# x1 transposed by DMA, its gain and shift on VectorE, the keys' statistics a block ahead, and the output's sums ahead of Q

## The chip, the cores and the metric

One of the eight cores of a Trainium2 chip runs the whole kernel; nothing is shared with another core. The metric is the time on the device in microseconds (us), as the median of several executions.

## What is computed

The input src is 4 batches of 2048 rows with 256 numbers. Each row is first normalized; then two branches are computed from it and multiplied:

```python
xn = _layernorm(src)
# branch 1: linear attention with 16 heads of 64, then a feed-forward net (FFN)
q = xn @ Wq + bq ; k = xn @ Wk + bk ; v = xn @ Wv + bv
Q = elu(q) + 1 ; K = elu(k) + 1
KV = einsum('bshd,bshm->bhdm', K, v)                    # a sum over all rows of the batch
Z = 1 / (einsum('bshd,bhd->bsh', Q, K.sum(axis=1)) + EPS)
o = einsum('bshd,bhdm,bsh->bshm', Q, KV, Z)
x1 = layer_norm(xn + o @ Wo + bo) * g1 + be1
y  = gelu(x1 @ W1 + b1) @ W2 + b2                       # 256 -> 1024 -> 256
s  = layer_norm(x1 + y) * g2 + be2
# branch 2: a gated net whose operands are rounded to FP4 in blocks of 16
g  = silu(fp4_linear(silu(fp4_linear(xn, w_gate)) * fp4_linear(xn, w_up), w_down))
out = src + s * g
```

All matrix products run in float32.

## The kernel before

**Blocks and batches.** The rows are taken in 32 blocks of 256 (two tiles j of 128 rows): 8 blocks in each of 4 batches. Attention of a batch needs sums over all of the batch's keys, so the keys of batch b + 1 are worked on beside the blocks of batch b. Each block of the first three batches (0 to 23) takes two key blocks along (`subs`). In blocks 0 to 3 of a batch, they are new: x is loaded (`x_k`), statistics are taken (`keys_stats`), x is normalized (`keys_norm`, the tile xn_k), stored, and transposed to xnT_k. In blocks 4 to 7 xn and xnT are read back from DRAM for the second half of the key columns. Keys are prepared one block ahead, so new ones are prepared in blocks 1, 2, 7 to 10 and 15 to 18 (and, a little differently, in block 0). In blocks 24 to 31 there are no keys left.

**The transposes of the keys** are done by DMA, in three steps. `keys_apart` has ScalarE copy the two 16-bit halves of each float32 number apart from each other (`apart<-xn_k`). A transposing DMA on SP's queue turns the eight 128x128 squares of 16-bit numbers (`apartT<-apart`). In `keys_T` one ScalarE copy puts the halves together again (`xnT_k<-apartT`).

**One block n of the loop**, in TensorE's order: keys times Wk (pk), the denominators of attention (pz), the sums of keys with xn (pxk), gate and up of block n + 1 (pg), down of block n (pd), the second key block's pk, attention of block n (pa, giving x1), the second pxk, W2's product of block n - 1 (py, 28 matmuls of 128x128, of which the trace records two passes each; a product of two 2x2 block matrices in seven multiplications instead of eight), and inside it, after its first 20 matmuls, the transposes of x1 (pt_x) and of the FP4 scales (pscale; in the last batch after 26), then Q of block n + 1 (pq) and W1's product of block n (pf). So x1 of block n has to be normalized and transposed between pa and pf.

**x1 before the change.** `attention_norm` takes the mean and variance on VectorE (`st`, `mv`), adds epsilon (`rstd`), raises to the power -1/2 on GpSimd (L430) and normalizes with one tensor_scalar for each tile. g1 and be1 are not in this x1: `x1_T` transposes it on TensorE with four 128x128 matmuls into PSUM, and ScalarE multiplies by g1 and adds be1 as columns when it copies the result to x1T. The same x1 in rows gets g1 and be1 + b2 (the row tile `shift`) later, in `ffn_addend` on GpSimd, so that it can be added to W2's product in `output`.

**The output of block n - 1.** `output` (called after Q of block n + 1 is issued) adds the product's seven partial sums to x1 with five VectorE additions (`add_seven`, into the tile s, reading PSUM), takes statistics of s, normalizes and gates it (`output_of`) and stores it.

**What sets the order.** TensorE's instructions stand in the order of the program (`keep_in_program_order`). Those of VectorE, ScalarE, GpSimd and SP's queue are placed by the framework's scheduler from the blocks on; `tc.issue_after(ins)` forbids it to place an instruction before another. Each engine and SP's queue of DMAs then works strictly in the order it got. PSUM has four banks for passing products (`mm_tile`); a product takes a bank that an earlier one has given back, so a late reader on ScalarE or VectorE can hold a later product. In Q, VectorE's clamp (`zq<-e,pq`, the maximum of product and clipped exponential) is such a reader.

Of the kernel before, what the change touches and what calls it, by code (L numbers as in the profile page):

```python
# [8 lines left out]
F32 = mybir.dt.float32  # L9
# [6 lines left out]
P = 128  # L16
# [6 lines left out]
def linear_attention_gated_by_fp4_ffn(  # L23
# [116 lines left out]
    def as_rows(v):  # L140
        return v.rearrange("(o f) -> o f", o=1).to_broadcast([P, v.shape[0]])
# [40 lines left out]
    for _ in range(24):  # L182
# [13 lines left out]
    W2_OF = {"11": 0, "21": 1, "22": 2, "t1": 3, "t2": 4, "t3": 5, "t4": 6}  # L196
    row_tiles = {
        name: const.tile([P, 1, D], F32, name=f"{name}_r")
        for name in ("bo", "g1", "shift", "g2", "be2")
    }  # L200
    rows = {name: t.to_broadcast([P, TB, D]) for name, t in row_tiles.items()}

# [3 lines left out]
    def load_row(name, v, dep):  # L206
        load_when(dep, row_tiles[name][:, 0, :], as_rows(v))
# [10 lines left out]
    def w2_sums():  # L218
# [23 lines left out]
            lambda dep: load_row("shift", be1, dep),  # L242
            lambda dep: load_row("g2", g2, dep),
            lambda dep: load_row("be2", be2, dep),
        ],
# [18 lines left out]

    cols = {}

    def add_b2(dep):
        b2_r = work.tile([P, D], F32, tag="s", name="b2_r", bufs=1)
        load_when(dep, b2_r, as_rows(b2))
        shift = row_tiles["shift"][:, 0, :]  # L270
        nc.gpsimd.tensor_tensor(shift, shift, b2_r, ALU.add)

    def small_constants():


        vs = (("b1", b1), ("g1", g1), ("be1", be1))
        n = sum(v.shape[0] // P for _, v in vs)
        brow = work.tile([n, P], F32, tag="z", name="brow", bufs=1)
        r = 0
        for name, v in vs:  # L280
            k = v.shape[0] // P
            nc.sync.dma_start(brow[r : r + k, :], v.rearrange("(c p) -> c p", p=P))
            cols[name] = (r, r + k)
            r += k
        yield
        pb = mm_tile("pb")
        tr(pb[:, :n], brow, ident[:n, :n])
        bcol = const.tile([P, n], F32, name="bcol")
        vector.tensor_copy(bcol, pb[:, :n])
        for name, (lo, hi) in cols.items():  # L290
            cols[name] = bcol[:, lo:hi]
        yield


# [2 lines left out]
    def fp4_scale(x, am, name):  # L297

        nb = x.shape[1]
        rs = small.tile([P, I // BLK], F32, tag="rs", name=f"rs_{name}")[:, :nb]  # L300
# [131 lines left out]
        ).ins  # L432
        return mv, rstd

    def normalize(dst, x, mv, rstd, js=range(TB)):
        for j in js:
            ins = vector.tensor_scalar(
                dst[:, j, :], x[:, j, :], mv[:, j, 0:1], rstd[:, j : j + 1],
                ALU.subtract, ALU.mult,
            )  # L440
        return ins.ins

    def transposes(x, name):

        pt = mm_tile(f"pt_{name}").rearrange("p (c t) -> p c t", c=ND)
        for c in range(ND):
            for j in range(TB):
                tr(
                    pt[:, c, j * P : (j + 1) * P], x[:, j, c * P : (c + 1) * P], ident
                )  # L450
        return pt

# [50 lines left out]
    def keys_apart(b, sub, issue=None):  # L503
# [7 lines left out]
        half = keys[b, sub][0].bitcast(U16).rearrange("p j (c f h) -> p h c j f", c=ND, h=2)  # L511
        apart = work.tile([P, 2, ND, TB, P], U16, tag="e", name=f"apart_{n}", bufs=3)
        with tc.issue_after(issue) if issue is not None else nullcontext():
            for h in range(2):
                scalar.copy(apart[:, h], half[:, h])
        apartT = work.tile([P, 2, ND * T], U16, tag="kk", name=f"apartT_{n}", bufs=3)
        nc.sync.dma_start(
            apartT.rearrange("p h (m t) -> p (h m) t", t=P),
            apart.rearrange("p h c j f -> p (h c j f)"),
            transpose=True,  # L520
        )
        keys[b, sub].append(apartT)

    def keys_T(b, sub, issue=None):

        f, bi = divmod(sub, NB)
        if f > 0:
            return
        n = b * NB + bi
        xn, *apartT = keys[b, sub]  # L530
        xnT = work.tile([P, ND, T], F32, tag="xnT_k", name=f"xnT_k_0_{n}", bufs=3)
        if apartT:
            with tc.issue_after(issue):
                scalar.copy(
                    xnT.bitcast(U16).rearrange("p c (t h) -> p h (c t)", h=2), apartT[0]
                )
# [53 lines left out]
    def in_seven(b):  # L590

        return b < B - 1
# [373 lines left out]
    def attention_norm(n, js=range(TB)):  # L966
        x1 = blk[n]["x1"]
        mv, rstd = stats(x1, f"1_{n}_{js[0]}", js)
        blk[n]["normal"] = normalize(x1, x1, mv, rstd, js)

    def x1_T(n):
        x1 = blk[n]["x1"]
        pt = transposes(x1, f"x1_{n}")
        x1T = work.tile([P, ND, T], F32, tag="x1T", name=f"x1T_{n}", bufs=1)
        for c in range(ND):
            ins = scalar.activation(
                x1T[:, c, :], pt[:, c, :], AF.Identity,
                bias=cols["be1"][:, c : c + 1], scale=cols["g1"][:, c : c + 1],
            )
        blk[n]["x1T"] = x1T  # L980
        blk[n]["act"] = ins.ins

    def ffn_1(n, chunks=range(NF)):
        x1T = blk[n]["x1T"]
# [40 lines left out]
    def output(n):  # L1025
# [4 lines left out]
        output_of(n, s, range(TB))  # L1030

    def output_of(n, s, js):
        g, o = blk[n]["g"], blk[n]["o"]
# [31 lines left out]
    for n in range(NB):  # L1065
# [47 lines left out]
        ready = weight  # L1113
        if n == 4:
            w_down_sb = load_down()
        if n == 5:
            add_b2(dep)
        if n == 6:
            load_xn(0)
            scales_x(0)  # L1120
# [49 lines left out]
    for n in range(NBLK):  # L1170
# [84 lines left out]
        bn, bin_ = divmod(n + 1, NB)  # L1255
        next_subs = (2 * bin_, 2 * bin_ + 1) if bn + 1 < B else ()
        for sub in next_subs if n > 0 else ():
            keys_in(bn + 1, sub)
        if n > 0:
            ffn_2(n - 1, 20)  # L1260
        more = n + 1 < NBLK, n + 2 < NBLK
        if more[0]:
            scales_h(n + 1, 0)
            behind = zs_ins if n == 0 else None if subs else qz_ins
            with tc.issue_after(behind) if behind is not None else nullcontext():
                scales_h(n + 1, 1)
            if more[1]:
                scales_x(n + 2)
        for sub in next_subs if n == 0 else ():
            with tc.issue_after(blk[n]["normal"]):  # L1270
                keys_in(bn + 1, sub)
        x1_T(n)
# [89 lines left out]
```

## Time and profile before

| | |
|---|---|
| median of 3 runs | 1881.18 us (1880.32 to 1881.52) |
| the profiled execution's own time | 1882.45 us |
| its span, first to last instruction | 1880.7 us |
| TensorE busy, matmuls | 1861.7 us, 99% |
| VectorE busy | 1363.6 us, 73% |
| ScalarE busy | 706.7 us, 38% |
| GpSimd busy | 386.9 us, 21% |
| SP's queue of DMAs, share of 16 engines' time | 47.4% |
| mean granted TensorE clock | 0.999 |

A line of the profile names the line of the kernel (L103 for all matmuls, L106 for transposes, L119 for everything of VectorE and ScalarE, because a helper records them there; so groups are told apart by their tiles), the engine, the operation, and out<-in by the names of the tiles. PE is TensorE, PEld its weight loads, DVE VectorE, ACT ScalarE, POOL GpSimd, SPq the queue of SP. In the timeline the first two numbers are start and duration in us; rows of equal instructions are merged. In brackets stands the idle time before an instruction and what ended it. A matmul's duration overlaps that of the next, so the step from start to start is what it takes of TensorE.

### The profile page before, as it was taken

The page shows a single profiled execution, that of the slowest core. Times are in us where ns is not written, and L with a number is a line of the kernel's source. Part 1 is how long each engine was busy: PE and PEld are TensorE (multiplying, and loading weights), DVE is VectorE, ACT ScalarE, POOL GpSimd, SP SyncE. Part 2 cuts the span into 40 slices and gives each one's busy share as a digit, 9 for nine tenths or more (in the row PEclk, how much of TensorE's full clock was granted, in tenths as well). Part 3 has the DMA queues.
Part 4 walks back from the last instruction along what each step waited for, and adds up shares of the span by engine and source line. Part 5 has one row for each costly group of instructions (what it writes and reads, how often), then busy time and mean ns, then how long its engine had stood idle before and what let it go on. Part 6 is the DMA issues. An engine that isn't in the chain of part 4 may idle for free.

```text
span 1880.7 us, 25219 instructions
## 1 busy us (share of the span) xinstructions
PE 1861.7 (99%) x9324; PEld 1383.0 (74%) x9324; DVE 1363.6 (73%) x2526; ACT 706.7 (38%) x1191; POOL 386.9 (21%) x371
## 2 busy tenths in 40 slices
PE   9999999999999999999999999999999999999998
PEld 4456677777777777777677787777777788888887
DVE  5676777766677877777667787776676767777775
ACT  2333544333334335443233533353322333333332
POOL 1411322011122212220112221122101122222212
PEclk9999999999999999999999999999999999999999
DMA  5526564434535456635344544564543544444442
GB/s 184 193 73 130 117 124 103 96 101 94 96 64 94 115 98 122 143 66 111 80 89 79 117 100 103 96 139 87 95 86 72 104 75 87 82 90 83 88 84 54
DMA packets 229434, 188.78 MB, mean 100 GB/s; under 512 B 107687, under 2 KB 191155, under 8 KB 229310
## 3 DMA queue, kind: packets, MB, share of 16 engines
q1 hardware_dynamic: 228476, 185.58, 47.4%
q8 instruction: 74, 1.21, 0.3%
q10 hardware_dynamic: 834, 1.58, 0.3%
q14 instruction: 50, 0.41, 0.1%
HBM read 131.96 MB, written 32.59 MB: 87 GB/s over the span
## 4 chain that ended last, share of the span: by engine, by line
PE 78%; DVE 11%; DMA 7%; issue 1%; POOL 1%; SPq 1%; ACT 1%; POOLq 0%; ACTq 0%; DVEq 0%
PE pg L103 13%; PE pf L103 11%; PE pk L103 10%; PE pxk L103 10%; PE pq L103 9%; PE pa L103 8%; PE pd L103 7%; PE py L103 7%; DMA zb<-z_d 3%; PE pz L103 2%; DMA z_d<-z 1%; DVE y L119 1%; DMA xn<-xn_d 1%; DVE x L119 1%; DVE hs L119 1%
## 5 line engine op out<-in xcount | busy, mean ns | idle before, releaser
L430 POOL TENSOR_TENSOR rstd<-rstd,neg_half 128x2 f32<-128x2 f32 (+1 forms) x98 | 77.8, 795 | 1298.0 <-DVE rstd L119 984.9
L103 PE MATMUL pg<-wgu,qT 128*128 128x352 f32 x1024 | 308.5, 459 | 0.1
L103 PEld LDWEIGHTS pg<-wgu,qT 128*128 128x128 f32 x1024 | 194.3, 190 | 113.7 <-issue 11.5
L103 PE MATMUL pk<-wk_sb,xnT_k 128*128 128x512 f32 x512 | 230.4, 592 | 1.2 <-ACT xnT_k L119 1.2
L103 PE MATMUL pq<-xnT,wq_sb 128*128 128x256 f32 x1024 | 227.6, 380 | 1.5 <-DVE zq L119 1.4
L103 PE MATMUL pxk<-kk,xn_k 128*128 128x512 f32 x496 | 227.9, 598 | 1.0 <-DVE kk L119 1.0
L103 PE MATMUL pf<-x1T,w_sb 128*128 128x256 f32 x1024 | 227.2, 380 | 1.1 <-DVE zq L119 0.6
L103 PEld LDWEIGHTS pf<-x1T,w_sb 128*128 128x128 f32 x1024 | 193.8, 190 | 30.4 <-DVE zq L119 4.0
L103 PEld LDWEIGHTS pq<-xnT,wq_sb 128*128 128x128 f32 x1024 | 191.8, 190 | 27.7 <-DVE zq L119 3.1
L119 DVE SCALAR_TENSOR_TENSOR kk<-ek,pk 128x512 f32<-128x512 f32 x128 | 85.6, 685 | 173.2 <-ACT ek L119 173.2
L103 PE MATMUL pd<-wd,qT 128*128 128x256 f32 x768 | 172.9, 380 | 0.0
L103 PEld LDWEIGHTS pk<-wk_sb,xnT_k 128*128 128x128 f32 x512 | 97.0, 190 | 102.6 <-issue 89.0
L119 ACT ACT_TABLE_LOAD x121 | 155.2, 1283 | 40.9 <-PE pk L103 26.0
L119 ACT ACTIVATE x1T<-pt_x,bcol 128x256 f32<-128x256 f32 x64 | 32.7, 561 | 359.3 <-PE pt_x L106 359.3
L103 PEld LDWEIGHTS pd<-wd,qT 128*128 128x128 f32 x768 | 145.3, 190 | 26.4 <-issue 2.5
L103 PEld LDWEIGHTS pxk<-kk,xn_k 128*128 128x128 f32 x496 | 89.4, 190 | 99.1 <-issue 87.3
L119 DVE TENSOR_TENSOR h<-h,pg 128x352 f32<-128x352 f32 x128 | 66.1, 517 | 107.1 <-PE pg L103 104.0
L119 ACT ACTIVATE h<-pg 128x352 f32<-128x352 f32 x128 | 58.9, 460 | 209.8 <-PE pg L103 209.7
L119 ACT ACTIVATE hT<-pf,bcol 128x256 f32<-128x256 f32 x256 | 106.1, 472 | 66.7 <-PE pf L103 66.3
L119 DVE TENSOR_TENSOR zq<-zq,zb 128x1024 f32<-128x1024 f32 x64 | 78.9, 1232 | 68.9 <-DMA zb<-z_d 68.8
L103 PE MATMUL py<-w_sb,hs 128*128 128x128 f32 x992 | 122.0, 275 | 0.0
L119 ACT ACTIVATE e<-pq,neg_one 128x512 f32<-128x512 f32 x128 | 86.2, 685 | 83.7 <-PE pq L103 71.2
(161 smaller groups left out, 2777.8 us busy)
## 6 DMA issues: line engine op xcount, KB each, us to landing
zb<-z_d SPq DMA_DIRECT2D x128, 256.0 KB, 6.2
qT<-scale_d SPq DMA_DIRECT2D x248, 128.0 KB, 6.0
x_k<-in_L_attn_src_dram SPq DMA_DIRECT2D x32, 256.0 KB, 4.1
x<-in_L_attn_src_dram SPq DMA_DIRECT2D x32, 256.0 KB, 2.9
xn_d<-xn_k SPq DMA_DIRECT2D x32, 256.0 KB, 2.5
xn<-xn_d SPq DMA_DIRECT2D x32, 256.0 KB, 2.7
xnT_d<-xnT_k SPq DMA_DIRECT2D x32, 256.0 KB, 2.0
xnT<-xnT_d SPq DMA_DIRECT2D x32, 256.0 KB, 4.3
```

The costliest lines, as they stand in the source:

```text
L103: return tc.keep_in_program_order(nc.tensor.matmul(*args, **kw))
L119: ins = op(*args, **kw)
L430: pool["last"] = nc.gpsimd.tensor_tensor(rstd[:, j0:j1], rstd[:, j0:j1], neg_half[:, j0:j1], ALU.pow).ins
```

## The change

Four things are edited.

1. In blocks 1 to 23 (`x1_by_dma`) x1 is transposed as the keys are: ScalarE copies the halves apart, a transposing DMA on SP's queue turns them, and a ScalarE copy in the middle of Q (`x1_together`, after the exponential of Q's second tile) puts them together. The halves lie in the tile of attention's sums (tag zs), which is free then; a third of it (`room`) takes the halves of the first key block. In blocks 0 and 24 to 31 the four transposes on TensorE stay, with one plain ScalarE copy after them.
2. g1 and be1 are applied to x1 in rows, on VectorE: two operations (subtract mean, times g1) and two (times rstd, plus be1) take the place of two tensor_scalar operations. `ffn_addend` then adds only b2, so that GpSimd has one operation fewer, and the column constants of g1 and be1 and the sum be1 + b2 fall away.
3. The statistics of new keys are taken a block earlier (`keys_stats_in`, at the end of a block's output, where W1's product runs); the keys' normalization is placed after x1's norm. The second key block's halves are copied apart after Q rather than before.
4. In blocks with keys the five additions of the output (`output_sums`) are given out ahead of Q instead of after it.

Its core:

```diff
+    def apart(x, xp, xpT):
+        half = x.bitcast(U16).rearrange("p j (c f h) -> p h c j f", c=ND, h=2)
+        for h in range(2):
+            ins = scalar.copy(xp[:, h], half[:, h])
+        nc.sync.dma_start(
+            xpT.rearrange("p h (m t) -> p (h m) t", t=P),
+            xp.rearrange("p h c j f -> p (h c j f)"),
+            transpose=True,
+        )
+        return ins.ins
+
+    def together(xT, xpT, issue):
+        with tc.issue_after(issue):
+            scalar.copy(xT.bitcast(U16).rearrange("p c (t h) -> p h (c t)", h=2), xpT)
...
+    def keys_stats_in(b, sub):
+        f, bi = divmod(sub, NB)
+        if f == 0:
+            keys[b, sub, "stats"] = keys_stats(b * NB + bi)
...
         if f == 0:
-            keys[b, sub] = [keys_norm(n, *keys_stats(n))]
+            st = keys.pop((b, sub, "stats"), None) or keys_stats(n)
+            keys[b, sub] = [keys_norm(n, *st)]
...
-            nc.gpsimd.tensor_tensor(x1, x1, rows["g1"], ALU.mult)
-            pool["last"] = nc.gpsimd.tensor_tensor(x1, x1, rows["shift"], ALU.add).ins
+            pool["last"] = nc.gpsimd.tensor_tensor(x1, x1, rows["b2"], ALU.add).ins
...
         mv, rstd = stats(x1, f"1_{n}_{js[0]}", js)
-        blk[n]["normal"] = normalize(x1, x1, mv, rstd, js)
+        for j in js:
+            vector.scalar_tensor_tensor(
+                x1[:, j, :], x1[:, j, :], mv[:, j, 0:1], rows["g1"][:, j, :], ALU.subtract, ALU.mult
+            )
+        for j in js:
+            ins = vector.scalar_tensor_tensor(
+                x1[:, j, :], x1[:, j, :], rstd[:, j : j + 1], rows["be1"][:, j, :], ALU.mult, ALU.add
+            )
+        blk[n]["normal"] = ins.ins
+
+    def x1_by_dma(n):
+        return n > 0 and in_seven(n // NB)
 
     def x1_T(n):
         x1 = blk[n]["x1"]
-        pt = transposes(x1, f"x1_{n}")
-        x1T = work.tile([P, ND, T], F32, tag="x1T", name=f"x1T_{n}", bufs=1)
-        for c in range(ND):
-            ins = scalar.activation(
-                x1T[:, c, :], pt[:, c, :], AF.Identity,
-                bias=cols["be1"][:, c : c + 1], scale=cols["g1"][:, c : c + 1],
-            )
+        x1T = blk[n]["x1T"] = work.tile([P, ND, T], F32, tag="x1T", name=f"x1T_{n}", bufs=1)
+        if x1_by_dma(n):
+            t = work.tile([P, 3, ND * T], F32, tag="zs", name=f"apart_x1_{n}", bufs=1).bitcast(U16)
+            xp, blk[n]["room"] = (
+                t[:, i].rearrange("p (h c j f) -> p h c j f", h=2, c=ND, j=TB) for i in (0, 2)
+            )
+            blk[n]["apart"] = t[:, 1].rearrange("p (h t) -> p h t", h=2)
+            blk[n]["act"] = apart(x1, xp, blk[n]["apart"])
+        else:
+            blk[n]["act"] = scalar.copy(x1T, transposes(x1, f"x1_{n}")).ins
+
+    def x1_together(n, issue):
+        if x1_by_dma(n):
+            together(blk[n]["x1T"], blk[n].pop("apart"), issue)
...
         for sub in next_subs if n > 0 else ():
-            keys_in(bn + 1, sub)
+            with tc.issue_after(blk[n]["normal"]):
+                keys_in(bn + 1, sub)
...
-        for sub in next_subs[: 1 if n == 0 else 2]:
-            keys_apart(bn + 1, sub, blk[n]["act"])
+        room = blk[n].pop("room", None)
+        for sub in next_subs[:1]:
+            keys_apart(bn + 1, sub, blk[n]["act"], room)
...
             ffn_2(n - 1, 28)
+            if subs:
+                output_sums(n - 1)
         if more[0]:
-            q_of(n + 1)
-        if n == 0:
-            keys_apart(bn + 1, next_subs[1], blk[1]["exp"])
+            q_of(n + 1, range(NH // 2))
+            x1_together(n, blk[n + 1]["exp"])
+            q_of(n + 1, range(NH // 2, NH))
...
         if n > 0:
-            output(n - 1)
+            if not subs:
+                output_sums(n - 1)
+            output_of(n - 1, blk[n - 1]["s"], range(TB))
...
         for sub in next_subs[:1]:
             keys_T(bn + 1, sub, blk[n + 1]["exp"])
+        for sub in next_subs[1:]:
+            keys_apart(bn + 1, sub, blk[n + 1]["exp"])
+        bn, bin_ = divmod(n + 2, NB)
+        for sub in (2 * bin_, 2 * bin_ + 1) if bn + 1 < B else ():
+            keys_stats_in(bn + 1, sub)
```

What is left out only follows from this: b2, be1 and g1 become row tiles, `small_constants` loads b1 alone, `add_b2` and `output` go, and the reciprocals' tiles (`rs`) have three buffers instead of four.

More of the change, by code (lines that the diff above doesn't have):

```diff
@@ L198, in linear_attention_gated_by_fp4_ffn @@
         name: const.tile([P, 1, D], F32, name=f"{name}_r")
-        for name in ("bo", "g1", "shift", "g2", "be2")
+        for name in ("bo", "g1", "be1", "b2", "g2", "be2")
     }
@@ L241, in linear_attention_gated_by_fp4_ffn @@
             lambda dep: load_row("g1", g1, dep),
-            lambda dep: load_row("shift", be1, dep),
+            lambda dep: load_row("be1", be1, dep),
+            lambda dep: load_row("b2", b2, dep),
             lambda dep: load_row("g2", g2, dep),
@@ L265, in linear_attention_gated_by_fp4_ffn @@
     cols = {}
[L267 to L271, printed above, removed]
-    def small_constants():
[L276 to L284, printed above, removed]
+    def small_constants():
+        brow = work.tile([NF, P], F32, tag="z", name="brow", bufs=1)
+        nc.sync.dma_start(brow, b1.rearrange("(c p) -> c p", p=P))
         yield
         pb = mm_tile("pb")
[L287 to L291, printed above, removed]
+        tr(pb[:, :NF], brow, ident[:NF, :NF])
+        cols["b1"] = const.tile([P, NF], F32, name="bcol")
+        vector.tensor_copy(cols["b1"], pb[:, :NF])
         yield
@@ L299, in fp4_scale @@
         nb = x.shape[1]
-        rs = small.tile([P, I // BLK], F32, tag="rs", name=f"rs_{name}")[:, :nb]
+        rs = small.tile([P, I // BLK], F32, tag="rs", name=f"rs_{name}", bufs=3)[:, :nb]
         vector.tensor_reduce(am, x, AX.X, ALU.max, apply_absolute_value=True)
@@ L433, in stats, with normalize @@
         return mv, rstd
-    def normalize(dst, x, mv, rstd, js=range(TB)):
-        for j in js:
-            ins = vector.tensor_scalar(
+    def normalize(dst, x, mv, rstd):
+        for j in range(TB):
+            vector.tensor_scalar(
                 dst[:, j, :], x[:, j, :], mv[:, j, 0:1], rstd[:, j : j + 1],
@@ L440, in normalize @@
             )
-        return ins.ins
     def transposes(x, name):
@@ L501, in keys_in, with keys_apart @@
             nc.sync.dma_start(xnT, xnT_d[n])
-    def keys_apart(b, sub, issue=None):
+    def keys_apart(b, sub, issue=None, xp=None):
         f, bi = divmod(sub, NB)
@@ L510, in keys_apart @@
         n = b * NB + bi
-        half = keys[b, sub][0].bitcast(U16).rearrange("p j (c f h) -> p h c j f", c=ND, h=2)
-        apart = work.tile([P, 2, ND, TB, P], U16, tag="e", name=f"apart_{n}", bufs=3)
+        if xp is None:
+            xp = work.tile([P, 2, ND, TB, P], U16, tag="e", name=f"apart_{n}", bufs=3)
+        apartT = work.tile([P, 2, ND * T], U16, tag="kk", name=f"apartT_{n}", bufs=3)
         with tc.issue_after(issue) if issue is not None else nullcontext():
[L514 to L520, printed above, removed]
-        )
+            apart(keys[b, sub][0], xp, apartT)
         keys[b, sub].append(apartT)
@@ L532, in keys_T @@
         if apartT:
[L533 to L536, printed above, removed]
+            together(xnT, apartT[0], issue)
         else:
@@ L968, in attention_norm @@
         mv, rstd = stats(x1, f"1_{n}_{js[0]}", js)
-        blk[n]["normal"] = normalize(x1, x1, mv, rstd, js)
+        for j in js:
[9 more added lines that the diff above has]
+        return n > 0 and in_seven(n // NB)
     def x1_T(n):
         x1 = blk[n]["x1"]
-        pt = transposes(x1, f"x1_{n}")
-        x1T = work.tile([P, ND, T], F32, tag="x1T", name=f"x1T_{n}", bufs=1)
-        for c in range(ND):
-            ins = scalar.activation(
-                x1T[:, c, :], pt[:, c, :], AF.Identity,
-                bias=cols["be1"][:, c : c + 1], scale=cols["g1"][:, c : c + 1],
-            )
-        blk[n]["x1T"] = x1T
-        blk[n]["act"] = ins.ins
+        x1T = blk[n]["x1T"] = work.tile([P, ND, T], F32, tag="x1T", name=f"x1T_{n}", bufs=1)
[3 more added lines that the diff above has]
+                t[:, i].rearrange("p (h c j f) -> p h c j f", h=2, c=ND, j=TB) for i in (0, 2)
+            )
+            blk[n]["apart"] = t[:, 1].rearrange("p (h t) -> p h t", h=2)
[5 more added lines that the diff above has]
+            together(blk[n]["x1T"], blk[n].pop("apart"), issue)
     def ffn_1(n, chunks=range(NF)):
@@ L1023, in ffn_2, with output_sums @@
         seven_products(blk[n]["py"], left, w2, order, lo, to)
-    def output(n):
+    def output_sums(n):
         x1, py = blk[n]["x1"], blk[n]["py"]
@@ L1029, in output @@
         add_seven(s, x1, py)
-        output_of(n, s, range(TB))
+        blk[n]["s"] = s
     def output_of(n, s, js):
@@ L1115, in linear_attention_gated_by_fp4_ffn @@
             w_down_sb = load_down()
-        if n == 5:
-            add_b2(dep)
         if n == 6:
@@ L1268, in linear_attention_gated_by_fp4_ffn @@
                 scales_x(n + 2)
+        x1_T(n)
         for sub in next_subs if n == 0 else ():
@@ L1271, in linear_attention_gated_by_fp4_ffn @@
                 keys_in(bn + 1, sub)
-        x1_T(n)
         if not subs:
@@ L1276, in linear_attention_gated_by_fp4_ffn @@
             gate_addend(n)
-        for sub in next_subs[: 1 if n == 0 else 2]:
-            keys_apart(bn + 1, sub, blk[n]["act"])
+        room = blk[n].pop("room", None)
+        for sub in next_subs[:1]:
+            keys_apart(bn + 1, sub, blk[n]["act"], room)
+        room = None
         if n > 0 and not subs:
```

## The prediction, before the changed kernel was run

> **What bounds the kernel now.** I read the page first (part 1), then the instructions on the tile of the x1 transposes, then TensorE's waits in blocks 1 to 23, then the timeline of one block, and last the same stretch of a block of the last batch.
>
> The page, and the transposes' tile (columns: duration of one in ns as min/median/max, first and last start):
>
> ```profile
> span 1880.7 us, 25219 instructions
> PE 1861.7 (99%) x9324; PEld 1383.0 (74%) x9324; DVE 1363.6 (73%) x2526; ACT 706.7 (38%) x1191; POOL 386.9 (21%) x371
> L106 PE MATMUL pt_x<-ident,x x128: 272/273/332, 192.1 to 1859.5; 128*128 128x128 f32 x128
> ```
>
> TensorE is busy for 99% of the span, so time is gained only by taking work or a wait off TensorE, and lost by giving it a wait. A matmul's 273 ns overlap the next one's, so the price of a transpose is the step from one start to the next. The timeline of block 15 (start, duration, both in us) gives it:
>
> ```profile
> 1047.66 2.84 PE L103 MATMUL py<-w_sb,hT 128*128 128x128 f32 x24
> 1050.34 1.95 PE L103 MATMUL py<-w_sb,hs 128*128 128x128 f32 x16
> 1052.12 0.60 PE L106 MATMUL pt_x<-ident,x 128*128 128x128 f32 x4
> 1052.56 0.27 PE L106 MATMUL pscale<-ident,scale 128*128 128x128 f32 x1
> 1052.67 1.95 PE L103 MATMUL py<-w_sb,hs 128*128 128x128 f32 x16
> 1054.45 5.34 PE L103 MATMUL pq<-xnT,wq_sb 128*128 128x256 f32 x24
> 1059.99 1.99 PE L103 MATMUL pq<-xnT,wq_sb 128*128 128x256 f32 x8 [0.19 <-DVE zq L119]
> ...
> 1061.82 0.59 PE L103 MATMUL pf<-x1T,w_sb 128*128 128x256 f32 x2
> ```
>
> Four transposes take 1052.56 - 1052.12 = 0.44 us of TensorE, 109 ns each. In some blocks they also wait for x1; TensorE's and its weight loads' waits between 200 and 1523 us (total, times, longest):
>
> ```profile
> PEld pt_x L106 <- DVE x L119: 3.4, 13, 0.6
> PEld pq L103 <- DVE zq L119: 3.1, 4, 1.6
> ```
>
> In the last batch, where the transposes stay, x1 comes just in time:
>
> ```profile
> 1600.64 0.17 DVE L119 TENSOR_SCALAR rstd<-mv 128x2 f32<-128x2 f32 x1
> 1600.89 0.70 POOL L430 TENSOR_TENSOR rstd<-rstd,neg_half 128x2 f32<-128x2 f32 x1 [22.37 <-DVE rstd L119]
> 1601.62 0.74 DVE L119 TENSOR_SCALAR x<-x,mv,rstd 128x256 f32<-128x256 f32 x2 [0.81 <-POOL rstd L430]
> 1602.28 0.68 PE L106 MATMUL pt_x<-ident,x 128*128 128x128 f32 x4
> 1602.80 1.50 PE L103 MATMUL py<-w_sb,hs 128*128 128x128 f32 x12
> ```
>
> Here the four take 0.52 instead of 0.44: TensorE already waits 0.08 us for the two normalizations.
>
> **The transposes leave TensorE in blocks 1 to 23.** From the last product before them to the first work after them, less that product's own 112 ns step, 15 blocks cost 0.44 us each and eight (5, 6, 12, 13, 14, 20, 21, 22) cost 0.67 to 1.29 with the wait: 6.55 + 7.43 = 13.98 us, of which 92 x 109 ns = 10.0 is work. All of it goes if the new path is on time.
>
> **Is the new x1T on time?** I lay the changed order on block 15's clock. x's statistics end at about 1047.8. Two operations with g1 follow, about 0.4 apart, with the 0.16 us addition between them; GpSimd's power takes 0.7 to 0.87; then two operations with be1 at 0.88 the pair (such a pair stands at 1615.65 of the trace): x1 is done at 1050.1, against 1049.84 now. ScalarE's two copies (apart now: 1.15 the pair) end at 1051.3. On SP's queue the transposing DMA stands behind the two stores of the keys' xn; their four normalizations at 0.37, no longer waiting for GpSimd, end at 1051.6, so it is issued at about 1052.0. The same kind of DMA, on tiles of the same size, lands here (us, min/median/max) in
>
> ```profile
> DMA to landing us min/median/max: 3.3/3.6/6.8
> ```
>
> so at 1055.6. The copy that joins the halves stands on ScalarE behind Q's second exponential. Q starts 0.44 earlier than now, at 1054.0; its second tile is done at 1057.5, the exponential (0.69) at 1058.2, the copy (1.33) at 1059.5. W1's product would start at 1054.0 + 32 x 0.216 = 1060.9. Slack 1.4 us; the landing may take 7.6 us before TensorE waits. The eight late x1's (at most 0.85 us) fit too.
>
> A rule of the Trainium skill speaks against the move: "VectorE: DVE Perf Modes", section Rules for kernel authors, wants 128x128 transposes on TensorE where PSUM will do as destination, and its section on the three transpose paths gives 390 ns on TensorE against 1309 ns by DMA. The row first: eight such squares land together in 3.6 us. By the page's figure taken one after another (my estimate) they would need 8 x 1.309 = 10.5 us, 2.9 too long, in 23 blocks 67 us lost. The row decides, and the 3.6 us lie beside other work while the 0.44 us on TensorE do not.
>
> **Sums of the output before Q.** They release a PSUM bank that Q's fourth tile takes, and hold Q's four clamps (zq) back on VectorE. On the same clock the last sum ends at 1057.4 and TensorE wants the bank at 1059.2; the clamps end at 1058.4, 1060.3, 1062.4, 1064.4 and W1's tiles want their banks at 1060.9, 1062.7, 1064.4, 1066.2. This includes 0.6 us in which the first output operation, now ahead of the third clamp, holds VectorE for GpSimd's power. Cover 1.8 us or more. The stalls in Q of blocks 2, 10 and 15 (1.40, 0.27, 0.35 between starts) had VectorE late there; I take 1.5 of the 2.0 as gone (bounds: 0 and 2.0).
>
> **The keys' statistics a block ahead.** Same instructions, later on VectorE, but they wait for x_k, which is loaded behind the new DMA. Issued at about 1053.5 and landing in 4.1 (its median), it is there at 1057.6, before its reader at 1059.2. In blocks 7 and 15 x_k is queued also behind the keys' own transposing DMA: issued at 1056.7, there at 1060.8; the clamps behind the waiting statistics come 1.6 late, the last at 1066.0 for 1066.2. I put +0.5 for the two (0 to +3).
>
> **The norm with g1 and be1, where the transposes stay (blocks 0, 24 to 31).** Before, after the statistics: addition, power, two normalizations. After: one g1 operation ahead of the addition (+0.40), and two be1 operations (0.88) for two normalizations (0.74). GpSimd's power runs beside the second g1 operation. "SBUF - State Buffer", section Who interferes with whom, says that a VectorE instruction with two SBUF inputs and a GpSimd one that reads SBUF hold each other off. The trace agrees in size only in part: beside such an operation the power took 0.87 instead of 0.70 (1614.75), so +0.16. By the row x1 is 0.40 + 0.16 + 0.1 = 0.65 later; by the rule's full hold (0.48) about 1.0. I take 0.65: TensorE has no slack, so 7 x 0.65 = +4.6 in blocks 24 to 30 and +0.65 in block 0. Block 31 shows no lateness (bounds 0 to +0.7), I take 0. Given back: W1's product waits 0.26 there for the first clamp in six blocks; that clamp has one sum fewer ahead of it (0.4) and one GpSimd operation of 1.27 fewer to collide with: -1.6.
>
> **At nothing:** ScalarE's work (x1T by one copy instead of two activations in the last batch; 2.5 us of copies for 1.0 elsewhere, at 38% load, Gelu still done 1 us before its reader); GpSimd's missing multiplication (21% busy); the constants (two loads of 1 KB fewer, one row load moved; if not covered, under 1 us). The 23 DMAs of 256 KB add 6 MB to 189, on queues busy 47%; the readers of the scales' transfers have some 2.5 us to spare.
>
> **The sum.** -13.98 - 1.5 + 0.5 + 4.6 + 0.65 - 1.6 = -11.3 us. The profiled execution took 1882.45 (span 1880.7 and 1.75 around it), so 1871.1; that execution stood 1.27 above the median 1881.18, so 1869.9 for the median. About 0.2% (3.8 us) is what a measurement of this kernel tells from no change.
>
> **The rivals.** *VectorE becomes late* in the ten blocks with keys to normalize and the eight of the last batch: for it, 73% load, cover under 2 us, collisions with GpSimd that I sized from single rows; against it, fewer waits for GpSimd ahead of the clamps. At 0.3 to 0.5 us more in 18 blocks, +5 to +9: 1875 to 1879. *The transposes' time comes back as another wait*: the eight late x1's had zb or the sums late before them, and TensorE may meet that lateness in pa or Q: the 3.95 us of waiting stay, and the 1.5 too: 1875. *Slower: the transposed x1 lands too late.* Its place is W1's product of each of 23 blocks, the price is landing time over 7.6 us, and the point from which it decides is 8.1 us, where 0.49 per block eats the gain. For it: the other transposing DMA of the same queue, of the quantized grid, lands in 2.7/7.8/9.3 us. At 9.3 that is 1.7 x 23 = 39, so 1909; at 8.5, 1890. Against it: that one is issued behind eight transfers that each copy a row of scales to 16 partitions, the new one behind two plain stores, as the keys' are.
>
> **How the numbers follow.** As summed: 0.72 (1864 to 1876). VectorE late or waits that come back: 0.17. Landing too late: 0.09; something else slower: 0.02. The range 1863 to 1880 takes the first two cases. Faster by over 0.2% (under 1877.4): 0.72 + 0.11 = 0.83; within 0.2%: 0.06; slower: 0.11.
>
> **What would show it.** Right: only 36 pt_x matmuls left; block period (W1 start to W1 start) 56.0 instead of 56.4 us where no half of M is made; x1T's DMA landing under 7 us; no wait of pf for x1T; in the last batch the wait of pt_x for x at about 0.6 to 0.7 us per block, period about 44.5 instead of 44.13. Wrong: pf or its weight loads waiting for ScalarE's x1T copy, waits of pf or Q for zq or s in the blocks with keys, or a last batch unchanged.

## The result, and the profile after

The change makes the kernel slower by a quarter of a per cent: 1883.99 us (1880.74 to 1887.07) against 1879.38 (1877.84 to 1881.52) of the kernel before on the same chip, ratio 1.0025 (95% interval 1.0016 to 1.0034). Taken again on another chip it was 1882.77 against 1878.49, 1.0023 (1.0014 to 1.0032). The forecast was 1870.

TensorE did lose the work. The page's first part, the row of the transposes' tile (count, min/median/max in ns), and the last line of the answer on the tile of x1's halves:

```profile
PE 1850.2 (98%) x9232; PEld 1370.6 (73%) x9232; DVE 1368.2 (73%) x2590; ACT 733.8 (39%) x1205; POOL 344.1 (18%) x338
```
```profile
L106 PE MATMUL pt_x<-ident,x x36: 272/273/331, 191.0 to 1859.5; 128*128 128x128 f32 x36
```
```profile
DMA to landing us min/median/max: 2.7/2.7/4.7
```

There are 92 matmuls fewer, and TensorE is busy for 11.5 us less in a span of the same 1880.7 us (the first profiled execution of before was one of its slower ones, 3.1 us above the median of 1879.38). The last row counts only landings that the trace shows: seven of the 23 transfers of x1, all of 2.73 to 2.76 us, and four of the keys' that use the same tile, of which the 4.7 is one. W1's product (pf) never waits for x1T. The period of a block in which TensorE waits for nothing is 56.01 us, before 56.44. So TensorE must wait for something new. Its waits and those of its weight loads between 200 and 1523 us (total, times, longest):

```profile
PE pf L103 <- DVE zq L119: 11.9, 10, 1.5
PE pq L103 <- DVE s L119: 2.7, 5, 1.1
```
```profile
PEld pf L103 <- DVE zq L119: 16.3, 12, 1.9
```

pf waits for Q's clamps (zq), up to 1.5 us at a time. In the kernel before, one such wait stood here:

```profile
PE pf L103 <- DVE zq L119: 0.6, 1, 0.6
```

The timeline of block 5 shows it (start, duration in us; in brackets the idle time and what ended it):

```profile
477.86 0.79 ACT L119 ACTIVATE m_h<-h 128x704 bf16<-128x704 f32 x1
...
478.67 0.89 DVE L119 SCALAR_TENSOR_TENSOR h<-m_h,h 128x704 f32<-128x704 bf16 x1 [1.44 <-ACT m_h L119]
...
479.48 0.68 DVE L119 TENSOR_TENSOR s<-x,py 128x512 f32<-128x512 f32 x1
...
485.77 3.62 PE L103 MATMUL pf<-x1T,w_sb 128*128 128x256 f32 x16
...
487.30 1.27 POOL L807 TENSOR_TENSOR o<-g,be_r 128x512 f32<-128x512 f32 x1
487.37 2.88 DVE L119 SCALAR_TENSOR_TENSOR o<-s,rstd,o 128x256 f32<-128x256 f32 x2 [0.58 <-POOL rstd L416]
...
488.65 1.32 POOL L808 TENSOR_TENSOR o<-o,x 128x512 f32<-128x512 f32 x1
...
490.18 1.27 DVE L119 SCALAR_TENSOR_TENSOR zq<-e,pq 128x512 f32<-128x512 f32 x2
...
490.90 1.35 PE L103 MATMUL pf<-x1T,w_sb 128*128 128x256 f32 x5 [1.51 <-DVE zq L119]
```

Two things are to be seen. First, VectorE idles 1.44 us for ScalarE's `m_h`, and the additions of the output (`s<-x,py`), whose product stood ready, are queued behind that wait. Second, both output operations (`o<-s,rstd,o`) stand ahead of the third and fourth clamp. They wait 0.58 us for GpSimd's power, and then take 2.88 us, 1.44 each, while GpSimd's gate addend (L807, L808) runs. The third tile of pf wants its bank at 485.77 + 16 x 0.216 = 489.2; the third clamp starts at 490.18. In block 5 of the kernel before, the same pair beside the same addend took as long, but behind the fourth clamp, where pf did not wait for it:

```profile
488.88 0.68 DVE L119 SCALAR_TENSOR_TENSOR zq<-e,pq 128x512 f32<-128x512 f32 x1
489.48 1.26 POOL L808 TENSOR_TENSOR o<-g,be_r 128x512 f32<-128x512 f32 x1
489.55 2.88 DVE L119 SCALAR_TENSOR_TENSOR o<-s,rstd,o 128x256 f32<-128x256 f32 x2
```

After the change, the chain of waits of this stretch names the output operations and the clamp:

```profile
486.48 0.86 POOL rstd L416
487.35 0.03 issue
487.37 2.88 DVE o L119 x2
490.25 0.61 DVE zq L119
```

To compare kernels I take one stretch of each profile, from the first pf matmul of block 0 to that of block 23, and in it TensorE's steps from one matmul's start to the next, less the usual step, where over 0.06 us are lost. Other losses are equal in all kernels or at most 0.8 us; only pa had 1.6 in the first profile of before.

| kernel | stretch, us | lost ahead of pf | of pq | of pt_x |
|---|---|---|---|---|
| before, two profiles | 1320.5, 1316.8 | 0.1, 0.2 | 2.5, 2.3 | 3.5, 1.5 |
| after, two profiles | 1320.2, 1320.9 | 13.2, 12.8 | 4.6, 5.3 | 0 |
| e1, outputs behind clamps | 1305.9 | 0.1 | 3.5 | 0 |
| e2, gate addend elsewhere | 1309.2 | 1.7 | 5.1 | 0 |
| e3, sums after Q | 1313.2 | 2.2 | 8.8 | 0 |
| e4, x1 on TensorE | 1315.4 | 0.1 | 0 | 1.9 |
| e6, sums ahead of the grid | 1303.8 | 0.4 | 1.2 | 0 |
| e9, m_h ahead of the halves | 1313.8 | 4.1 | 7.2 | 0 |
| e15, e6 with statistics in place | 1308.9 | 0.2 | 6.4 | 0 |

From after to e6 the lost time falls by 16.2 us and the stretch by 16.4: what TensorE waited is what the change lost.

### The profile page after: what moved, and what is told of

It reads as the page before. It is cut to its first block, busy times and chain, and to the rows that moved or that the text cites. A ratio compares the mean times of both kernels' runs of the same rounds, so it can differ in the third digit from the quotient of the medians.

```text
span 1880.7 us, 25130 instructions
## 1 busy us (share of the span) xinstructions
PE 1850.2 (98%) x9232; PEld 1370.6 (73%) x9232; DVE 1368.2 (73%) x2590; ACT 733.8 (39%) x1205; POOL 344.1 (18%) x338
## 4 chain that ended last, share of the span: by engine, by line
PE 65%; DVE 15%; DMA 10%; issue 6%; POOL 1%; SPq 1%; ACT 1%; POOLq 0%; DVEq 0%; ACTq 0%
PE pg L103 10%; PE pf L103 10%; PE pxk L103 9%; PE pk L103 9%; PE pq L103 7%; PE pa L103 7%; PE pd L103 5%; PE py L103 5%; DMA zb<-z_d 4%; DMA z_d<-z 2%; DVE x L119 2%; DMA xn<-xn_d 2%; DVE zq L119 2%; PE pz L103 1%; DVE hs L119 1%
## 5 line engine op out<-in xcount | busy, mean ns | idle before, releaser
L119 DVE SCALAR_TENSOR_TENSOR kk<-ek,pk 128x512 f32<-128x512 f32 x128 | 85.6, 684 | 183.7 <-ACT ek L119 183.7
L119 DVE TENSOR_TENSOR h<-h,pg 128x352 f32<-128x352 f32 x128 | 66.0, 516 | 101.9 <-PE pg L103 98.7
L119 ACT ACTIVATE h<-pg 128x352 f32<-128x352 f32 x128 | 58.9, 460 | 198.6 <-PE pg L103 198.6
L119 ACT ACTIVATE hT<-pf,bcol 128x256 f32<-128x256 f32 x256 | 105.1, 474 | 67.4 <-PE pf L103 66.7
L119 DVE TENSOR_TENSOR zq<-zq,zb 128x1024 f32<-128x1024 f32 x64 | 80.8, 1267 | 67.5 <-DMA zb<-z_d 67.4
L119 ACT ACTIVATE e<-pq,neg_one 128x512 f32<-128x512 f32 x128 | 86.8, 687 | 101.1 <-PE pq L103 100.0
L119 ACT ACTIVATE ek<-pk,neg_one 128x512 f32<-128x512 f32 x128 | 85.5, 686 | 84.0 <-PE pk L103 79.7
```

The source lines that it names most:

```text
L119: ins = op(*args, **kw)
```

## The experiments

All ratios are to the kernel before, run on the same chip, with 95% intervals. Theory A: the output operations ahead of the clamps, beside GpSimd's addend, make the loss (to which a second condition, A2, was added after the first four). Rivals: VectorE is overloaded and the lateness only moves; the DMA path itself costs. The times expected count from a kernel before of 1879.4 us; it took 1877.4 to 1878.5 on the chips of the experiments, so the ratios are the better comparison.

**e1: the output operations behind Q's last clamp, in blocks with keys.** The diffs below show the core of each edit.

```diff
-        for j in js:
-            vector.scalar_tensor_tensor(
-                o[:, j, :], s[:, j, :], rstd[:, j : j + 1], o[:, j, :], ALU.mult, ALU.add
-            )
+        with tc.issue_after(behind) if behind is not None else nullcontext():
+            for j in js:
+                vector.scalar_tensor_tensor(
+                    o[:, j, :], s[:, j, :], rstd[:, j : j + 1], o[:, j, :], ALU.mult, ALU.add
+                )
...
-            output_of(n - 1, blk[n - 1]["s"], range(TB))
+            output_of(n - 1, blk[n - 1]["s"], range(TB), blk[n + 1]["clamp"] if subs else None)
```

> Edit: the changed kernel, with the two output operations (o<-s,rstd,o) held behind Q's fourth clamp in blocks with keys; nothing else moves. Theory A (the loss is those two operations standing ahead of the third and fourth clamp, each 1.44 us long beside GpSimd's gate addend): the stalls of pf for zq, 12.1 us in nine blocks, go, and little takes their place: 1884.0 - 12.1 + 0 to 2 = 1872 to 1874, 0.3 to 0.4% faster than the kernel before. Rival B (VectorE is loaded too much; the lateness moves): pf's waits shrink by less than half, or waits of pz, pa or pq appear in their place: 1879 to 1884. Rival C (the DMA path of x1 slows other transfers or TensorE without a visible wait): pf's waits go, but the time stays above the kernel before by some us, with longer steps between matmuls.

Measured: 1869.64 against 1877.37, 0.9955 (0.9943 to 0.9968). In the timeline of its block 5:

```profile
487.02 1.28 DVE L119 SCALAR_TENSOR_TENSOR zq<-e,pq 128x512 f32<-128x512 f32 x2
...
488.22 2.36 DVE L119 SCALAR_TENSOR_TENSOR o<-s,rstd,o 128x256 f32<-128x256 f32 x2
```

The clamps no longer wait, and the outputs are as slow as ever (2.36), but nobody waits for them. This one order turns a loss of 0.25% into a gain of 0.45%. The rivals would have left 1879 or more.

**e2: GpSimd's gate addend at another time, VectorE's order unchanged.**

```diff
-        if 1 < n < last and subs:
-            gate_addend(n - 1)
...
-            if n == 1:
+            if n > 0:
                 gpsimd_behind(keys[b + 1, subs[0]][-1][0])
                 gate_addend(n - 1)
```

> Edit: the changed kernel, with GpSimd's gate addend (L807 to L809) of block n-1 held behind the first key block's kk in every block with keys, so that it runs at another time than the output operations; VectorE's order stays. Theory A in its full form (collision): the output operations take 0.48 us each instead of 1.44, 1.9 us less ahead of the third and fourth clamp, more than the largest stall of 1.69; the stalls of pf go: 1872 to 1875. If the order alone were to blame and the collision not: the pair stays near 2.9 us, and so do the stalls and the time, 1884. Rival B: the addend now meets other VectorE work, and waits appear there: 1878 to 1884.

Measured: 1871.91 against 1877.37, 0.9968 (0.9956 to 0.9979). The outputs stand where they stood in the changed kernel, and the pair takes 0.88 us instead of 2.88:

```profile
488.63 0.88 DVE L119 SCALAR_TENSOR_TENSOR o<-s,rstd,o 128x256 f32<-128x256 f32 x2 [0.58 <-POOL rstd L416]
489.43 1.28 DVE L119 SCALAR_TENSOR_TENSOR zq<-e,pq 128x512 f32<-128x512 f32 x2
```

pf started at 487.04 there and wants the bank at 490.5; the third clamp is done at 490.1. In none of the blocks with this order does pf wait any more. The 1.7 us that e2 still loses ahead of pf stand in block 15 (1.6), where the clamps are late for another reason, VectorE's wait for a load of keys:

```profile
1056.34 0.43 DVE L119 BATCH_NORM_STATS2 st<-x_k 128x6 f32<-128x256 f32 x1 [3.50 <-DMA x_k<-in_L_attn_src_dram]
```

So the order alone costs pf nothing here; the order together with the collision costs 13 us.

**e3: the additions after Q again (the fourth part undone).**

```diff
-            if subs:
-                output_sums(n - 1)
...
-            if not subs:
-                output_sums(n - 1)
+            output_sums(n - 1)
```

> Edit: the changed kernel with the fourth part undone alone: the five additions of the output are given out after Q again. Theory A: the output operations then stand behind the clamps as before, pf's waits for zq go (-12.1), and Q's waits for the sums' bank come back to about the 2.0 us that the kernel before had (-1.7 against 3.7 now): 1870 to 1874. Rival B (the statistics a block ahead or the loads make VectorE late): waits of pf or pq stay: 1878 to 1884.

Measured: 1877.79 against 1877.37, 1.0003 (0.9995 to 1.0011). Half a miss: pf's waits went as expected, but Q's did not come back to 2.0 us, they became 8.8 (table):

```profile
PE pq L103 <- DVE s L119: 6.4, 9, 1.5
PE pf L103 <- DVE zq L119: 1.3, 1, 1.3
```

The 1.44 us wait for `m_h` is there in this kernel too (`h<-m_h,h` at 1393.09 with `[1.44 <-ACT m_h L119]`), the additions now stand behind all of the grid's operations, and the fourth tile of Q waits 1.09 for its bank. So the fourth part is needed. The scheduler also left only one output operation ahead of the third clamp in this run; in block 5 it took 1.48 us, and pf lost 0.34 instead of 1.8. This run led to A2.

**e4: x1 transposed on TensorE in all blocks (the first part undone).**

```diff
     def x1_by_dma(n):
-        return n > 0 and in_seven(n // NB)
+        return False
```

> Edit: the changed kernel with x1 transposed on TensorE in all blocks (the first part's DMA undone, the rest kept). Theory A: TensorE gets 23 x 0.44 = 10 us of work back, and waits of pt_x for an x1 that comes later than before by 0.65 us in these blocks (0 to 10 us), while the output operations still collide (12 us, less the 0.44 by which pf starts later: 23 blocks' stalls shrink by up to 4): 1888 to 1900. Rival C (the DMA path costs what it gains): 1880 to 1885.

Measured: 1878.12 against 1877.37, 1.0002 (0.9994 to 1.0010), 10 us below what A expected; it would look like rival C. The timeline says why not. Without the DMA, the scheduler put two additions ahead of `h<-m_h,h`, where the changed kernel has none, and left both output operations behind the third clamp (487.19):

```profile
479.02 0.68 DVE L119 TENSOR_TENSOR s<-x,py 128x512 f32<-128x512 f32 x1
...
479.74 0.55 DVE L119 TENSOR_TENSOR s<-s,py 128x384 f32<-128x384 f32 x1
...
480.71 0.89 DVE L119 SCALAR_TENSOR_TENSOR h<-m_h,h 128x704 f32<-128x704 bf16 x1 [0.42 <-ACT m_h L119]
```

VectorE's wait shrinks from 1.44 to 0.42, and the first clamp starts 3.7 us ahead of pf (484.05 to 487.75) instead of 1.6 (484.20 to 485.77). The edit changed two things, and A2 had to be tested with the DMA left in.

**e6: the DMA kept, the additions ahead of the grid.**

```diff
-            grid_of_h(n + 1, 1, blk[n]["act"])
+            h_ins = grid_of_h(n + 1, 1, blk[n]["act"], blk[n - 1].get("second") if subs and n > 0 else None)
...
-                grid_of_x(n + 2, blk[n]["act"])
+                grid_of_x(n + 2, blk[n]["act"], h_ins if subs and n > 0 else None)
```

The new argument holds the grid's operations on VectorE (`issue_after`) behind the second addition, and those of x behind the first of h.

> Edit: the changed kernel, with VectorE's grid operations of h (h<-m_h,h) held behind the second of the output's five additions, and those of x (y<-m_x,y) behind the first of h's. Theory A2 (a second condition of the loss: VectorE idles 1.44 us for ScalarE's m_h, which stands behind the two copies of x1's halves, and the additions, whose product is there before, stand behind that wait): filling the wait makes the clamps 1.2 us earlier; the stalls of pf fall from 12.1 to 0 to 4 us and those of Q from 3.7 to under 1: 1870 to 1875. In some blocks the scheduler then also splits the two output operations around the third clamp. Rival A1 (only the output operations' place and collision matter): the stalls of pf fall by less than 3 us and the time stays at 1880 to 1884.

Measured: 1867.39 against 1878.02, 0.9944 (0.9931 to 0.9956).

```profile
476.69 0.68 DVE L119 TENSOR_TENSOR s<-x,py 128x512 f32<-128x512 f32 x1
...
477.40 0.55 DVE L119 TENSOR_TENSOR s<-s,py 128x384 f32<-128x384 f32 x1
...
478.22 0.89 DVE L119 SCALAR_TENSOR_TENSOR h<-m_h,h 128x704 f32<-128x704 bf16 x1 [0.26 <-ACT m_h L119]
...
485.82 1.48 DVE L119 SCALAR_TENSOR_TENSOR o<-s,rstd,o 128x256 f32<-128x256 f32 x1 [0.58 <-POOL rstd L419]
...
487.22 0.68 DVE L119 SCALAR_TENSOR_TENSOR zq<-e,pq 128x512 f32<-128x512 f32 x1
```

Two additions fill VectorE's wait, the output operation still takes 1.48 us ahead of the third clamp, and the clamp is done at 487.90, 0.8 us before pf wants the bank (485.28 + 3.46 = 488.74). One thing is not separated here: the scheduler also put the second output operation (0.89) behind the third clamp, in all 13 blocks in which the changed kernel had both ahead of it beside the addend. With it in front, the clamp would have been about on time or late by up to 0.6 us, by the two durations seen (0.89 and 1.44); that order was not run. So e6 does not show that the wait for `m_h` alone costs pf anything; e3 kept that wait, split the two operations, and lost 2.2 us there. What the wait costs is seen in Q: e1 keeps all 13 waits (18.5 us of VectorE) and loses 3.5 us ahead of pq, e6 is left with nine of 0.3 us or less (2.3) and loses 1.2.

e6 and e4 have a similar order on VectorE and differ in the way of x1: 1315.4 - 1303.8 = 11.6 us in the stretch, 0.9944 against 1.0002. Of this, 92 x 0.109 = 10.0 us are the transposes themselves, the rest is a balance of waits (1.9 ahead of pt_x and 0.8 of pa in e4, 1.6 of pq and pf in e6). So the DMA path gains its 10 to 12 us, which refutes rival C.

**e9: m_h ahead of the copies of the halves.**

```diff
-            grid_of_h(n + 1, 1, blk[n]["act"])
+            grid_of_h(n + 1, 1, None if x1_by_dma(n) else blk[n]["act"])
```

> Edit: the changed kernel, with m_h of the second half (m_h<-h on ScalarE) no longer held behind the copies of x1's halves, so that it stands ahead of them. Theory A2: VectorE's wait of 1.44 us is gone from another side, the additions and clamps come 1 us or more earlier, with the output operations left ahead of the third and fourth clamp: stalls of pf 0 to 4 us, of Q under 1: 1870 to 1875. Rival A1: stalls of pf stay near 12 us, 1881 to 1884. If x1 comes later because of the operation that moves ahead of it, waits of pf for x1T or of pa appear.

Measured: 1877.06 against 1878.02, 0.9995 (0.9989 to 1.0002). A miss. The wait for m_h became another one; VectorE's waits between 257.7 and 1520 us:

```profile
DVE y L119 <- ACT m_x L119: 14.2, 22, 1.3
...
DVE h L119 <- ACT m_h L119: 4.3, 5, 0.9
```

The operation of x's grid (`y<-m_x,y`) now stands first, in many blocks ahead of the additions, and waits for `m_x`, which ScalarE makes only after the halves. That agrees with A2 (what counts is whether the additions stand in front of VectorE's wait for ScalarE, not for which tile it waits), but does not prove it: the order of outputs and clamps changed too, and two of the largest losses in Q (1.2 and 1.9 us, in blocks 8 and 16) have no such wait over 0.6 us ahead of them.

**e11: e1 with the norm of before in blocks 24 to 31** (the second part undone there: `tensor_scalar` twice on VectorE, g1 and be1 on ScalarE and GpSimd).

```diff
+        if not in_seven(n // NB):
+            for j in js:
+                ins = vector.tensor_scalar(
+                    x1[:, j, :], x1[:, j, :], mv[:, j, 0:1], rstd[:, j : j + 1],
+                    ALU.subtract, ALU.mult,
+                )
+            blk[n]["normal"] = ins.ins
+            return
```

> Edit: the kernel of e1 (output operations behind the clamps), with the norm of x1 in blocks 24 to 31 as before the change (two tensor_scalar on VectorE, g1 and be1 as columns on ScalarE, the gain on GpSimd). It tests the second part by itself. By the profile after: the period of a block of the last batch goes from 44.34 back to 44.13 us, the stretch of the four transposes from 1085 to some 520 ns, and the time falls by 7 x 0.21 = 1.5 us against e1: ratio to the kernel before 0.9947 for 0.9955. By the prediction's own sum it would be 4.6 less 1.6 = 3.0 us: 0.9939. If the additional operation of GpSimd meets the clamps, nothing is gained.

Measured: 1869.10 against 1878.02, 0.9949 (0.9937 to 0.9962); the interval holds e1's 0.9955 too, so the time alone proves nothing. The profiles agree with the expectation: the period is 44.13 again, and the stretch from pf of block 23 to the second part of pf of block 30 (which TensorE takes in two parts) falls from 316.1 to 314.6 us, by 1.5. Up to pf of block 31 it is 1.8 (340.76 to 338.95).

**before_again and after_again: second profiles.**

> The kernel before, unchanged, for a second profile. The first profiled execution stood 3 us above the median. If its eight waits of pt_x for x1 (3.95 us) are typical, they are there again, with 0.7 to 1.3 us of stretch in about eight blocks; if they belonged to that execution, they are under 2 us, and the transposes' gain shrinks from 13.98 to 10 to 12 us.

> The changed kernel, unchanged, on the same chip as the repairs and for a second profile. Theory A: the stalls of pf for zq in blocks of types 4 to 6 are typical of it: seven to nine of 1.6 to 1.7 us again, 11 to 13 us in all, ratio to the kernel before 1.002 to 1.003. If they belonged to the one execution that was profiled, they differ by several us.

The second profile of before (1877.10 us) has less waiting of the transposes; its weight loads' waits, where the first profile had 3.4 us:

```profile
PEld pt_x L106 <- DVE x L119: 1.5, 7, 0.4
```

Beyond 0.436 us each, the transposes took 1.8 us in all, not 3.95. The waits after the change are typical, though with five stalls of 1.7 us and two of 1.3 rather than the seven to nine that were expected:

```profile
PE pf L103 <- DVE zq L119: 11.5, 9, 1.5
PE pq L103 <- DVE s L119: 3.4, 7, 1.0
```

**e13 and e14: the repairs together.** e13 is e6 with e11's norm; e14 has e1's edit as well.

> The version that the runs point to: e6 (the additions ahead of the grid's operations) with the norm of e11 in blocks 24 to 31. The two edits lie in different batches and should add: 0.9944 - 0.0008 = 0.9936, near 1866 us where the kernel before takes 1878.

> e13 with the output operations also held behind the clamps (as in e1). If either repair alone clears the loss, as theory A with its two conditions says, the second adds nothing: within 0.1% of e13. If the splitting of the two output operations in e6 still costs something (0.25 us in one block by its profile), it gains that.

Measured: e13 1868.07, 0.9948 (0.9935 to 0.9960); e14 1866.28, 0.9939 (0.9926 to 0.9951), both against 1878.49. e14 is the fastest version by its median, 16.5 us (0.9%) below the changed kernel on the same chip; e6, e13 and e14 cannot be told apart by their intervals, and e13 did not reach the 0.9936 that was expected. In its profile 1.1 us are won against e6 in the last batch (the stretch used for e11), and 1.7 are lost in block 7 (period 60.51 against 58.82), where VectorE waits for x_k, the load that the statistics a block ahead need, and two clamps stand behind it:

```profile
598.70 0.43 DVE L119 BATCH_NORM_STATS2 st<-x_k 128x6 f32<-128x256 f32 x1 [2.90 <-DMA x_k<-in_L_attn_src_dram]
599.04 0.67 DVE L119 SCALAR_TENSOR_TENSOR zq<-e,pq 128x512 f32<-128x512 f32 x1
...
599.77 1.99 PE L103 MATMUL pf<-x1T,w_sb 128*128 128x256 f32 x8 [0.56 <-DVE zq L119]
```

**e15: e6 with the statistics of the keys in their own block (the third part undone, but for the second key block's copies, which stay behind Q).**

```diff
-            with tc.issue_after(blk[n]["normal"]):
-                keys_in(bn + 1, sub)
+            keys_in(bn + 1, sub)
...
-        bn, bin_ = divmod(n + 2, NB)
-        for sub in (2 * bin_, 2 * bin_ + 1) if bn + 1 < B else ():
-            keys_stats_in(bn + 1, sub)
```

> e6 with the third part undone: the statistics of new keys are taken in the block that normalizes them again, ahead of the grid and the sums (some 2 us of VectorE in the ten blocks with new keys). It tests the prediction's +0.5 us (0 to +3) for that part. By that sum this kernel would be 0 to 3 us faster than e6: 0.993 to 0.9944. Theory A, by which lateness of VectorE ahead of Q's clamps is what costs, says the opposite: waits of Q for s or of pf for zq appear in blocks with keys, and it is 2 to 12 us slower than e6: 0.9955 to 1.0008.

Measured: 1872.39 against 1878.49, 0.9970 (0.9957 to 0.9982), 5.1 us more than e6 in the stretch, all of it in Q:

```profile
PE pq L103 <- DVE s L119: 4.8, 7, 1.5
```

The third part is worth 5 us in e6's order; the prediction had it as a small cost.

## Why the prediction was wrong, point by point

**The transposes leave TensorE: right, mis-sized.** 36 are left and the period is 56.01, as forecast. The term of 13.98 us held 3.95 of waiting from a single execution; a second one showed 1.8, so the term is 11.8, near the 11.6 between e4 and e6.

**x1T on time: right.** 2.7 us to landing in the seven transfers that the trace shows, where 3.6 was taken, and no wait of pf for x1T in any block; the rival *the transposed x1 lands too late* did not come. The estimate of 10.5 us for eight squares, from the Trainium skill's "VectorE: DVE Perf Modes", section The three transpose paths, falls to the measurement of 2.7.

**Sums ahead of Q: the step that failed.** The prediction wrote of "0.6 us in which the first output operation, now ahead of the third clamp, holds VectorE for GpSimd's power" and "Cover 1.8 us or more". It had laid this out on block 15. There it holds: in the changed kernel that block's output operations stand one on each side of the third clamp, take 0.48 each, and pf does not wait. The lines of block 15 after the change:

```profile
1058.41 7.07 PE L103 MATMUL pf<-x1T,w_sb 128*128 128x256 f32 x32
...
1060.52 0.48 DVE L119 SCALAR_TENSOR_TENSOR o<-s,rstd,o 128x256 f32<-128x256 f32 x1 [0.58 <-POOL rstd L416]
...
1060.92 0.68 DVE L119 SCALAR_TENSOR_TENSOR zq<-e,pq 128x512 f32<-128x512 f32 x1
...
1061.52 0.48 DVE L119 SCALAR_TENSOR_TENSOR o<-s,rstd,o 128x256 f32<-128x256 f32 x1
```

But 13 blocks (2 to 5, 10 to 13, 18 to 22), in which no statistics of new keys stand between the clamps, have another order: both operations ahead of the third clamp, and GpSimd's addend beside them. There they hold VectorE for 0.58 + 2.88 = 3.46 us, not 0.6, and in ten of them pf loses 0.1 to 1.8 us. Blocks 6, 14 and 23 have both operations ahead of the clamp without the addend (0.48 each), and pf does not wait. The price stood in the trace of before, in the row of the output's tile:

```profile
L119 DVE SCALAR_TENSOR_TENSOR o<-s,rstd,o x62: 476/1478/1493, 260.9 to 1867.8; 128x256 f32<-128x256 f32 x62
```

The median is 1478 ns, three times the minimum: most of them already ran beside GpSimd's operations, at no cost to pf, because they stood behind the clamps. The Trainium skill's "SBUF — State Buffer", section Who interferes with whom, which the prediction applied to the power alone, says it of these operations too: an instruction of VectorE with two SBUF inputs contends with a GpSimd one that reads SBUF. e2, which takes away the overlap and leaves VectorE's order, agrees: 0.88 us for the pair instead of 2.88. So where the sum had -1.5, pf lost 13 us more than before and Q 2.1 to 2.9.

**Q's stalls** were to fall by 1.5. Those in blocks 2, 10 and 15 did go, as forecast, but new ones of 4.6 us came: 0.5 in block 16, 2.8 in the blocks without keys to normalize, where the additions were queued behind VectorE's wait for `m_h` (between 257.7 and 1520 us, total, times, longest):

```profile
DVE h L119 <- ACT m_h L119: 18.5, 13, 1.4
```

Another 1.3 stand in block 1 and stay in e1, e2 and e6; their cause is open. The prediction read where the additions went relative to the clamps, not relative to the grid.

**The keys' statistics a block ahead: right in its mechanism, wrong in its value.** The waits for x_k in blocks 7 and 15 came (1.0 and 2.0 us; 1.6 was forecast), and cost pf at most 0.1 in the changed kernel, but 1.6 in e2, 1.7 in e13 and 1.0 in e14, within 0 to 3. That the part takes 5 us of lateness out of Q was not seen.

**The norm with g1 and be1.** In the last batch the transposes stretch by 0.57 us per block (0.65 forecast) and the six waits of pf for zq vanish (-1.6, as forecast); the period is 44.34, forecast 44.5, before 44.13. The sum of +3.0 us is +1.5 to 1.8 by e11. From pf of block 23 to pf of block 31 the kernels before (340.3 and 340.5) and after (340.9 and 340.5) hardly differ, since a wait of one block of before (block 26, period 45.4 and 45.6; its transposes took 1.29 us) is gone. Block 0 lost 0.57 in the transposes, and pf's wait there grew from 0.6 to 1.3 us (the one wait of pf in e3's row above).

**The rivals.** *VectorE becomes late* named the right engine and wait, but looked for it in the ten blocks with keys to normalize. All stalls of 1 us and more are in blocks without. Its 0.3 to 0.5 us per block were 1.7 in the worst six.

**The sum again**, for the stretch, with measured terms between the two second profiles: -11.8 (transposes) + 12.7 (pf) + 2.9 (Q) + 0.2 (pa) = +4.0; measured 1320.9 - 1316.8 = +4.1. With the order repaired (e1) the time is 0.9955 of before, nearly what was forecast (0.994). In part that is luck: the sum had 15.0 us gained in this stretch, where e1 gained 10.9 (1316.8 to 1305.9), and 3.0 lost in the last batch, where it lost 0.3 to 0.4 (to pf of block 31).

## What to carry to other kernels

When a change frees an engine that is busy 99% of the time, the order on the next engine decides what arrives: check what stands between its reader and the bank in *every kind of block*, not in the one that is convenient to lay out. Price an operation by the spread of its row, not by its minimum: here a median at three times the minimum meant that it usually ran beside something, and moving it onto the path brought that price along. And where a queue waits for another engine, see whether ready work stands behind the wait; here two additions put in front of it (with which one output also fell behind the third clamp), or both outputs put behind the clamps, each turned +0.25% into about -0.5%.

## What the runs showed of the hardware that was not expected

- A VectorE operation with two SBUF inputs of 128x256 took 0.48 us alone and 1.47 to 1.50 beside GpSimd's 128x512 operations of about 1.3 us: the pair took 2.88, and its second ended 0.28 us after the GpSimd operation that it met (block 5, 490.25 against 489.97).
- Eight 128x128 squares of 16 bits turned by one DMA landed in 2.7 us in the seven of 23 that the trace shows, where the same kind of DMA on the keys had taken 3.6 in the kernel before (median of the six of 22 shown). The keys' own took longer after the change, 5.4 (ten of 22), without a wait of TensorE for them.
- The load x_k of block 7, issued within 0.1 us of the same time in e6 and e13, was there for its reader after 3.2 us in one and 4.8 in the other; that of block 15 took 5.1 in e2. A cover of 4 us would have been enough in the first and not in the others.
